# A hybrid state-space and attention kernel: another pacing of the recurrence, and the carry copies on another engine

## The chip, the cores and the metric

The kernel runs on one core of a Trainium2 chip, as one launch. The core has a matrix engine (TensorE, PE in the profile), a vector engine (VectorE, DVE), a scalar engine (ScalarE, ACT), a general one (GpSimd, POOL) and a queue engine (SyncE, SP) that issues most transfers here. [...] The metric is the time of one execution on the device in microseconds (us), as the median over runs. A change of less than 0.5% can't be told from none.

## The reference

The input is eight images of 384 channels and 32 x 32 positions. All arithmetic is in float32. Two layers follow each other.

- Layer 0: an RMS norm over channels, then a selective state-space recurrence over the 1024 positions, once forwards and once backwards, and a 3 x 3 depthwise convolution with a sigmoid gate. The recurrence is `h = dA * h + dBu`, and its output at a position is the sum over 16 states of `h * c`. There are 384 channels x 16 states of it per image and direction.
- Layer 1: a layernorm, causal attention with six heads of 64 over 1024 positions, and, for the first five images only, a second layernorm and a feed-forward part from 384 to 1536 to 384 channels with weights made binary in five groups. Both of its matrix products are scaled by the largest absolute value of the whole image, so the quantised GELU can't begin before the last element of the first product is there.

```
def step(h, inp):
    dA, dBu, c = inp
    h = dA * h + dBu
    return (h, jnp.einsum('bdn,bn->bd', h, c))
```

## The kernel before

**Stages of one image.** `before_scan` (line 308) computes everything that the recurrence reads: norm, input projection (line 342), the short convolution (370 or, on TensorE, 372), the local 3 x 3 convolution with its gates (`local`, 384; `gates`, 445), and `delta` (515), which writes the step sizes and inputs to DRAM. The recurrence follows in slots, and then `attention` (678) and, for five of the images, `feed_forward` (970).

**The recurrence.** It is cut into 768 units, 96 per image: a unit is one group of 128 channels, one half of the positions, one direction and two states. POOL first multiplies the input by the rows of B (`s_first`, line 592). ACT makes the decay factors (line 605), DVE runs two scans of 512 elements (line 610), POOL multiplies the result in place by the rows of C (line 616), and TensorE adds it to a PSUM bank by eight transposing matmuls (line 624). Between the two halves of a direction the last value of each state is carried: the first half copies it into a small tile (line 615), and the second half's scans start from it. So 384 of the 768 units have that copy; before the change POOL makes it, between its two multiplications. POOL's instructions are pinned to program order (`pin`), and a unit's first multiplication is issued two slots ahead of its scans. Six buffers hold `g`.

**The order of the work.** The program is a list of steps, each with a time in us that the author gives it (`Steps`, default 2.5; `@emit.of(...)` sets another). `spread_over` (1084) merges lists in proportion to these times. The tile framework then turns the list into engine queues, with the list's order as priority. The kernel has three parts.

- Part one (0 to 831 us): the input stages of four images and the making of the binary weights, with the first 98 slots spread evenly over them.
- Part two (831 to 4741 us): `rest`, built in lines 1149 to 1158. For each of seven images the attention steps come first. For four of the images a joint list follows: its feed-forward merged with the input stage of a later image, every time multiplied by `JOINT` (0.6). Images 5 and 6 have attention alone. The seventh (image 4) has a feed-forward with no input stage left to merge. Lines 1160 to 1171 then place the slots: each image's 96 slots have to be issued by the end of the stage before its attention, and of the stretches that keep this, the one with the most slots per planned us is taken first, evenly spaced. The planned times therefore decide how many slots fall beside each kind of step; they don't change any step.
- Part three (4741 to 4951 us): the attention of image 7, with no recurrence left.

**The steps that the change touches.** `layernorm` (281) has four steps of 6.0 each. In `attention`, the values (line 745) and the steps of softmax have the default of 2.5: `scores` (773) with the matmuls of line 787, the masking on DVE (801) and the exponential (811), and the steps of `weighted_values` with the transposes (863), their copies (866) and the products with the values (877). There are 36 + 42 = 78 such steps in an image. In `feed_forward`, the two scalings (1011 and 1057) and GELU (1018, 1021) have 3.0 each; TensorE has nothing to do for that image in them.

Of the kernel before, what the change touches and what calls it, by code (L numbers as in the profile page):

```python
# [38 lines left out]
BC0 = 32  # L39
DW = BC0 + 2 * NS  # L40
PARTS = ((0, 0), (0, 1), (1, 1), (1, 0))
JOINT = 0.6
SET = 8
HURRY = 400
AHEAD = 2
# [9 lines left out]
def kernel(  # L55
# [16 lines left out]
    nc = tc.nc  # L72
    pin = tc.keep_in_program_order
# [13 lines left out]
    def btile(name):  # L87
        return big.tile([P, NC, L], F32, name=name, tag="big")
# [16 lines left out]
    def half(h):  # L105
        return slice(h * HB, (h + 1) * HB)
# [153 lines left out]
    def mean_of(c_of, name):  # L260

        m = bank(name)
        for c in range(NC):
            nc.tensor.matmul(out=m, lhsT=onesc, rhs=c_of(c), start=(c == 0), stop=(c == NC - 1))  # L264
        return m
# [6 lines left out]
    def squares(src, h, name):  # L272
        sqs = []
        for c in range(NC):
            if c % 2 == 0:
                sq = mtile(f"sq_{name}_{h}_{c}").rearrange("p (i l) -> p i l", i=2)
            nc.scalar.activation(sq[:, c % 2, :], src[:, c, half(h)], AF.Square)
            sqs.append(sq[:, c % 2, :])
        return sqs

    def layernorm(src, name, emit):

        dst = src
        st = {}
        for h in range(NH):

            @emit.of(6.0)
            def _(h=h):
                mean = mean_of(lambda c: src()[:, c, half(h)], f"mean_{name}_{h}")
                for c in range(NC):  # L290
                    nc.vector.tensor_tensor(
                        dst()[:, c, half(h)], src()[:, c, half(h)], mean, ALU.subtract
                    )
                st[h] = squares(dst(), h, name)

        for h in range(NH):

            @emit.of(6.0)
            def _(h=h):
                var = mean_of(lambda c: st[h][c], f"var_{name}_{h}")  # L300
                rstd_of(var, 1)
                for c in range(NC):
                    nc.vector.tensor_tensor(  # L303
                        dst()[:, c, half(h)], dst()[:, c, half(h)], var, ALU.mult
                    )
# [289 lines left out]
    def s_scan(u):  # L595
        g = sst["g", u.name]
        key = ("carry", u.b, u.c, u.d)
        begins = u.part % 2 == 0
        if begins and u.n == 0:
            sst[key] = sp.tile([P, NS], F32, name=f"carry_{u.name}", tag="carry", bufs=2 * NC)  # L600
        carry = sst[key]
        for i in range(2):
            n = u.n + i
            da = bank(f"da_{u.name}_{i}", "da")
            nc.scalar.activation(  # L605
                da, sst["dl", u.b, u.c, u.part], AF.Exp, scale=amat[:, u.c, n : n + 1]
            )
            first = 0.0 if begins else carry[:, n : n + 1]
            gi, step = g[:, i, :], -1 if u.d else 1
            nc.vector.tensor_tensor_scan(  # L610
                gi[:, ::step], da[:, ::step], gi[:, ::step], first, ALU.mult, ALU.add
            )
        if begins:
            end = 0 if u.d else HB - 1
            pin(nc.gpsimd.tensor_copy(carry[:, u.n : u.n + 2], g[:, :, end]))  # L615
        pin(nc.gpsimd.tensor_tensor(g, g, sst["bc", 1, u.b, u.part, u.n], ALU.mult))  # L616

    def s_sum(u):
# [59 lines left out]
    def attention(b, emit_ffn, emit):  # L678
# [57 lines left out]
                        nc.any.tensor_copy(st["qk"[s]][:, m, half(h)], qp)  # L736
        for j in range(NT):

            @emit
            def _(j=j):  # L740
                if j == 0:
                    st["v"] = btile(f"v_{b}").rearrange("p c l -> p (c l)").rearrange(
                        "p (j e) -> p j e", e=C
                    )
                vp = bank(f"vp_{b}_{j}")
                for c in range(NC):
                    nc.tensor.matmul(  # L747
                        out=vp[:, :C],
                        lhsT=st["xn"][:, c, chunk(j)],
                        rhs=wv[:, c, :],  # L750
                        start=(c == 0),
                        stop=(c == NC - 1),
                    )
                nc.any.tensor_copy(st["v"][:, j, :], vp[:, :C])
# [13 lines left out]
        def probabilities(c, g, steps):  # L768


            nb = g + 1

            def scores(i, qi, n, kb, k0, k1):
                pr = mtile(f"pr_{b}_{c}_{qi}_{kb}").rearrange("p (e l) -> p e l", e=2)
                st["pr", c, g, i, kb] = pr
                if kb == 0 and i == 0:
                    for what in ("nm", "rs"):
                        st[what, c, g] = small.tile(
                            [P, QT, 2, nb], F32, name=f"{what}_{b}_{c}_{g}", tag=f"{what}{nb}"
                        )  # L780
                nm, rs = st["nm", c, g], st["rs", c, g]
                ss = [bank(f"s_{b}_{c}_{qi}_{kb}_{e}", "s") for e in range(2)]

                order = (1, 0)
                for e in order:
                    with at_once(e == order[1]):
                        mm = nc.tensor.matmul(  # L787
                            out=ss[e][:, : k1 - k0],
                            lhsT=st["q"][rows_of(e), c, chunk(qi)],
                            rhs=st["k"][rows_of(e), c, k0:k1],  # L790
                            start=True,
                            stop=True,
                        )
                    if e == order[1]:
                        pin(mm)

                w = k1 - k0
                mask = cmask[:, HB - w :] if k1 == n else cmask[:, :1].to_broadcast([P, w])
                for e in range(2):
                    x, m = pr[:, e, :w], nm[:, i, e, kb : kb + 1]  # L800
                    nc.vector.tensor_tensor_reduce(  # L801
                        out=x,
                        in0=ss[e][:, :w],
                        in1=mask,
                        scale=-1.0,
                        scalar=-MASKED,
                        op0=ALU.add,
                        op1=ALU.min,
                        accum_out=m,
                    )  # L810
                    nc.scalar.activation(  # L811
                        x, x, AF.Exp, bias=m, scale=-1.0, accum_out=rs[:, i, e, kb : kb + 1]
                    )

            for i in range(QT):
                qi = g * QT + i
                n = (qi + 1) * P
                for kb, (k0, k1) in enumerate(blocks_of(n)):
                    steps(lambda i=i, qi=qi, n=n, kb=kb, k0=k0, k1=k1: scores(i, qi, n, kb, k0, k1))

        def weighted_values(c, g, steps):

# [72 lines left out]

            for j in range(last + 1):

                @steps
                def _(j=j):
                    if j == 0:  # L900
                        with tc.high_priority(offset=60):
                            factors()
                    if j % QT == QT - 1:
                        spread(j // QT)
                    turned(j)
                    if j > 0:
                        weigh(j - 1)

            @steps
            def _():  # L910
                weigh(last)

# [57 lines left out]
    def feed_forward(b, t, emit):  # L970
# [35 lines left out]
                            st["mxh"][:, m : m + 1], hm, AX.X, ALU.max, apply_absolute_value=True  # L1006
                        )

        @emit.of(3.0)
        def _():  # L1010
            st["s1"] = quant_scale(st["mxh"], f"h_{b}")


        @emit.of(3.0)
        def _():
            with tc.high_priority(offset=60):
                for q in range(NF // NC):
                    pin(nc.scalar.activation(st["h", q], st["h", q], AF.Gelu, scale=st["s1"]))
                pin(nc.scalar.preload_act_table_set(LOG_EXP))
                for q in range(NF // NC):  # L1020
                    nc.vector.tensor_scalar(st["h", q], st["h", q], QCLIP, None, ALU.min)  # L1021
# [30 lines left out]
                            st["mxy"][:, m : m + 1], ym, AX.X, ALU.max, apply_absolute_value=True  # L1052
                        )

        @emit.of(3.0)
        def _():
            st["s2"] = quant_scale(st["mxy"], f"y_{b}")

# [16 lines left out]
    class Steps(list):  # L1075
# [4 lines left out]

        def of(self, us):
            return lambda f: self(f, us)

    def spread_over(*lists):

# [64 lines left out]
    for i, b in enumerate(ORDER):  # L1150
        if i > 0:
            due.append((sum(us for _, us in rest), i * per))
        fed = Steps()
        rest += steps_of(attention, b, fed) if i < B - 1 else []
        if fed and later:
            fed = spread_over(fed, steps_of(before_scan, later.pop(0), ("pt", "pt", "av")))
            fed = [(f, JOINT * us) for f, us in fed]
        rest += fed

    timed, here = [], 0  # L1160
# [63 lines left out]
```

## Time and profile before

| | |
|---|---|
| Median of 3 runs | 4947.5 us (4943.6 to 4969.1) |
| Profiled execution: time, span | 4952.4 us, 4950.6 us |
| Granted TensorE clock, mean | 0.885 |
| Busy: PE, DVE, ACT, POOL | 81%, 74%, 54%, 75% |
| A joint stage, mean of four | 324.5 us |
| An attention stage with the recurrence beside it | 329 to 357 us |
| The last attention, without it | 210 us |
| The last feed-forward (image 4) | 212 us |

The profile is of one execution. A row of it names the line, the engine, the operation, what it writes and reads and how often it ran; then come the busy time in us and the mean of one in ns; then how long the engine was idle just before, and who ended that idle time. An answer by windows gives, for each stretch of time, its length and the busy us of each engine in it with the number of instructions. Busy time of PE is of pipelined matmuls whose ends are modelled.

### The profile page before, as it was taken

The numbers are of one execution on the slowest core, as the hardware profiler recorded it, in microseconds if no ns is written. First come the engines' busy times: TensorE is split into PE (matmuls) and PEld (weight loads), VectorE is DVE, ScalarE is ACT, GpSimd is POOL, SyncE is SP. The second block draws the span as 40 slices with busy tenths as digits, with TensorE's granted clock in tenths as the row PEclk, the third lists the DMA queues.
The fourth block names the chain that finished last, engine by engine and source line by source line (L and its number), as shares of the span: only waits on it lengthen the run. The fifth ranks groups of instructions, "written<-read, shape, count | busy, mean of one in ns | idle before, by whom it ended". The sixth has DMA issues, their size and how long they took to land. (4 is left out here: it accounts for less than half of the span.)

```text
span 4950.6 us, 50616 instructions
## 1 busy us (share of the span) xinstructions
PE 4007.3 (81%) x16362; PEld 2168.0 (44%) x16362; DVE 3659.0 (74%) x4818; ACT 2669.5 (54%) x4855; POOL 3696.7 (75%) x1944
## 2 busy tenths in 40 slices
PE   4677786988788788688887888887887988988889
PEld 1243343544444444344443444443454444444444
DVE  6887878677887778786778967687867677676623
ACT  4565655564654655545655446565456365464425
POOL 0487787996878986768876699867799888888800
PEclk7787796999989899888898998898899989989999
DMA  6554546333454334363343634334643334334210
GB/s 228 204 177 165 196 157 238 107 102 124 150 198 137 115 124 165 126 207 114 108 135 128 220 121 135 111 128 153 203 128 119 114 112 140 117 103 139 92 61 26
DMA packets 365009, 696.35 MB, mean 141 GB/s; under 512 B 30104, under 2 KB 88904, under 8 KB 364744
## 3 DMA queue, kind: packets, MB, share of 16 engines
q1 hardware_dynamic: 355232, 676.97, 41.4%
q10 hardware_dynamic: 9512, 16.15, 0.9%
q8 instruction: 129, 2.11, 0.2%
q14 instruction: 136, 1.11, 0.1%
HBM read 527.33 MB, written 165.68 MB: 140 GB/s over the span
## 5 line engine op out<-in xcount | busy, mean ns | idle before, releaser
L592 POOL TENSOR_TENSOR g<-ud,bc 128x1024 f32<-128x1024 f32 x768 | 1843.2, 2400 | 518.7 <-PE y L624 391.9
L616 POOL TENSOR_TENSOR g<-g,bc 128x1024 f32<-128x1024 f32 x768 | 1821.0, 2371 | 271.1 <-DVE g L610 196.1
L605 ACT ACTIVATE da<-dl,amat 128x512 f32<-128x512 f32 x1536 | 1056.9, 691 | 1457.7 <-DVE g L610 1436.7
L610 DVE TENSOR_TENSOR_SCAN g<-da,g 128x512 f32<-128x512 f32 x768 | 907.5, 1211 | 423.5 <-POOL g L592 411.8
L610 DVE TENSOR_TENSOR_SCAN g<-da,carry,g 128x512 f32<-128x512 f32 x768 | 953.7, 1272 | 348.4 <-POOL g L592 322.9
L624 PE MATMUL y<-ident,g 128*128 128x128 f32 x6144 | 938.7, 301 | 249.2 <-POOL g L616 122.2
L624 PEld LDWEIGHTS y<-ident,g 128*128 128x128 f32 x6144 | 782.0, 155 | 696.7 <-issue 379.8
L787 PE MATMUL s<-k,q 64*128 64x512 f32 (+3 forms) x1152 | 388.4, 600 | 121.6 <-DVE nm L801 103.5
L801 DVE CUSTOM_DVE_ANT_0 pr<-s,cmask 128x512 f32<-128x512 f32 (+3 forms) x576 | 300.3, 546 | 168.4 <-PE s L787 167.1
L811 ACT ACTIVATE pr<-pr,nm 128x512 f32<-128x512 f32 (+3 forms) x576 | 349.9, 609 | 123.6 <-DVE nm L801 121.9
L863 PE MATMUL pt<-ident,pr 128*128 128x128 f32 x1728 | 301.9, 307 | 98.1 <-ACT ptn L866 78.5
L995 PE MATMUL hp<-t,w 128*128 128x512 f32 x720 | 335.7, 611 | 38.7 <-DMA w<-w1s 30.8
L1039 PE MATMUL yp<-h,w 128*128 128x512 f32 x720 | 331.7, 619 | 19.2 <-DMA w<-w2s 15.1
L863 PEld LDWEIGHTS pt<-ident,pr 128*128 128x128 f32 x1728 | 216.2, 154 | 240.2 <-ACT ptn L866 134.5
L877 PE MATMUL av<-ptn,v 128*64 128x512 f32 (+3 forms) x1152 | 270.8, 551 | 49.7 <-ACT ptn L866 35.8
L342 PE MATMUL in<-xn,win 128*128 128x512 f32 x576 | 282.7, 637 | 26.8 <-DVE xc L464 8.2
L866 ACT COPY ptn<-pt 128x512 f32<-128x512 f32 (+3 forms) x576 | 255.6, 474 | 62.0 <-PE pt L863 60.0
L401 DVE SCALAR_TENSOR_TENSOR loc<-xn,vec,loc 128x496 f32<-128x496 f32 (+3 forms) x384 | 259.6, 722 | 20.1 <-ACT loc L390 18.8
L729 PE MATMUL qp<-t,wqk 128*128 128x512 f32 x576 | 263.3, 607 | 10.3 <-DVE t L303 6.5
L615 POOL COPY carry<-g 128x2 f32<-128x2 f32 x384 | 85.7, 223 | 214.8 <-DVE g L610 214.6
L787 PEld LDWEIGHTS s<-k,q 64*128 64x128 f32 x1152 | 132.2, 207 | 257.9 <-DVE nm L801 174.9
L1039 PEld LDWEIGHTS yp<-h,w 128*128 128x128 f32 x720 | 141.8, 201 | 194.0 <-issue 169.8
(151 smaller groups left out, 4714.2 us busy)
## 6 DMA issues: line engine op xcount, KB each, us to landing
bc<-rows SPq DMA_DIRECT2D x512, 512.0 KB, 4.2
dl<-sdl SPq DMA_DIRECT2D x160, 256.0 KB, 3.0
ud<-sud SPq DMA_DIRECT2D x160, 256.0 KB, 2.8
t<-st SPq DMA_DIRECT2D x63, 512.0 KB, 5.0
su<-u SPq DMA_DIRECT2D x48, 512.0 KB, 4.0
du<-su SPq DMA_DIRECT2D x96, 256.0 KB, 3.9
sdl<-du SPq DMA_DIRECT2D x96, 256.0 KB, 2.6
sud<-du SPq DMA_DIRECT2D x96, 256.0 KB, 2.2
```

The lines of the kernel that those rows point to most:

```text
L342: nc.tensor.matmul(out=mp, lhsT=st["win", c][:, k, i, :], rhs=st["xn"][:, k, half(h)], start=(k == 0), stop=(k == NC - 1),)
L592: pin(nc.gpsimd.tensor_tensor(g, ud, sst["bc", 0, u.b, u.part, u.n], ALU.mult))
L605: nc.scalar.activation(da, sst["dl", u.b, u.c, u.part], AF.Exp, scale=amat[:, u.c, n : n + 1])
L610: nc.vector.tensor_tensor_scan(gi[:, ::step], da[:, ::step], gi[:, ::step], first, ALU.mult, ALU.add)
L616: pin(nc.gpsimd.tensor_tensor(g, g, sst["bc", 1, u.b, u.part, u.n], ALU.mult))
L624: nc.tensor.matmul(out=y[:, j, :], lhsT=g[:, i, chunk(j)], rhs=ident, is_transpose=True, start=(u.opens and i == 0 and j == 0), stop=(u.cl ...
L787: mm = nc.tensor.matmul(out=ss[e][:, : k1 - k0], lhsT=st["q"][rows_of(e), c, chunk(qi)], rhs=st["k"][rows_of(e), c, k0:k1], start=True, st ...
L801: nc.vector.tensor_tensor_reduce(out=x, in0=ss[e][:, :w], in1=mask, scale=-1.0, scalar=-MASKED, op0=ALU.add, op1=ALU.min, accum_out=m,)
L811: nc.scalar.activation(x, x, AF.Exp, bias=m, scale=-1.0, accum_out=rs[:, i, e, kb : kb + 1])
L863: nc.tensor.transpose(pt[:, chunk(i)], pr[:, e, chunk(j % QT)], ident)
L995: nc.tensor.matmul(out=hp, lhsT=st["w1"][:, c, chunk(m % 2)], rhs=st["xn"][:, c, half(h)], start=(c == 0), stop=(c == NC - 1),)
L1039: nc.tensor.matmul(out=yp, lhsT=st["w2", k // 6][:, k % 6, :], rhs=st["h", k // NC][:, k % NC, half(h)], start=(k == 0), stop=(k == NF - 1),)
```

## The change

The planned times are set anew, and one copy moves.

- `JOINT` is 1.0 instead of 0.6, so a joint list counts with its full planned time.
- The steps of softmax are planned at 1.6 instead of 2.5, the values at 2.0 instead of 2.5, the layernorm steps at 3.0 instead of 6.0.
- The two scalings and GELU are of a new type `Gap`, with 9, 16 and 9 instead of 3 each. In a joint list these times are used when the feed-forward and the input stage are merged; after that each counts as `SHORT`, 3.0, in the placing of slots. In the last feed-forward they count in full.
- The copy of the carried values is issued to VectorE instead of GpSimd, and isn't pinned to program order there.

```diff
-JOINT = 0.6
+JOINT = 1.0
+SHORT = 3.0
...
-            @emit.of(6.0)
+            @emit.of(3.0)
             def _(h=h):
                 mean = mean_of(lambda c: src()[:, c, half(h)], f"mean_{name}_{h}")
...
-            @emit.of(6.0)
+            @emit.of(3.0)
             def _(h=h):
                 var = mean_of(lambda c: st[h][c], f"var_{name}_{h}")
...
             end = 0 if u.d else HB - 1
-            pin(nc.gpsimd.tensor_copy(carry[:, u.n : u.n + 2], g[:, :, end]))
+            nc.vector.tensor_copy(carry[:, u.n : u.n + 2], g[:, :, end])
         pin(nc.gpsimd.tensor_tensor(g, g, sst["bc", 1, u.b, u.part, u.n], ALU.mult))
...
-            @emit
+            @emit.of(2.0)
             def _(j=j):
                 if j == 0:
                     st["v"] = btile(f"v_{b}").rearrange("p c l -> p (c l)").rearrange(
...
-                    steps(lambda i=i, qi=qi, n=n, kb=kb, k0=k0, k1=k1: scores(i, qi, n, kb, k0, k1))
+                    steps(lambda i=i, qi=qi, n=n, kb=kb, k0=k0, k1=k1: scores(i, qi, n, kb, k0, k1), 1.6)
...
-                @steps
+                @steps.of(1.6)
                 def _(j=j):
...
-            @steps
+            @steps.of(1.6)
             def _():
                 weigh(last)
...
-        @emit.of(3.0)
+        @emit.of(Gap(9.0))
         def _():
             st["s1"] = quant_scale(st["mxh"], f"h_{b}")
...
-        @emit.of(3.0)
+        @emit.of(Gap(16.0))
         def _():
             with tc.high_priority(offset=60):
                 for q in range(NF // NC):
...
-        @emit.of(3.0)
+        @emit.of(Gap(9.0))
         def _():
             st["s2"] = quant_scale(st["mxy"], f"y_{b}")
...
+    class Gap(float):
+        pass
+
...
-            fed = [(f, JOINT * us) for f, us in fed]
+            fed = [(f, JOINT * (SHORT if isinstance(us, Gap) else us)) for f, us in fed]
         rest += fed
```

## The prediction

> **What bounds the kernel now.** I read the page's first two parts, then busy time by stage, then the softmax stretches, then single rows. The page says that no engine is full over the span:
>
> ```profile
> PE 4007.3 (81%) x16362; PEld 2168.0 (44%) x16362; DVE 3659.0 (74%) x4818; ACT 2669.5 (54%) x4855; POOL 3696.7 (75%) x1944
> ```
>
> So the stages differ. With the stages cut at the first and last out-projection matmuls of each image (lines 699, 937), three windows show the two kinds and the attention that runs with no recurrence beside it (columns: PE, PEld, DVE, ACT, POOL busy us, then granted clock, DMA share, GB/s):
>
> ```profile
> 1486.00:1830.00 344.00, 285.92 (x1376) 162.18 (x1376) 252.18 (x365) 186.63 (x396) 303.21 (x156) 0.91 0.39 128
> 1830.00:2159.00 329.00, 258.17 (x873) 134.88 (x872) 265.28 (x291) 183.61 (x266) 226.74 (x118) 0.88 0.47 153
> 4741.00:4951.00 210.00, 199.70 (x864) 95.41 (x864) 66.12 (x201) 98.06 (x258) 0.00 (x0) 0.98 0.09 35
> ```
>
> Attention (first line) has POOL at 0.88 and DVE at 0.73; the joint stage (second) has DVE at 0.81, PE 0.78, POOL only 0.69. The softmax part shows the first more sharply, with and without the recurrence:
>
> ```profile
> 1590.00:1810.00 220.00, 175.55 (x1004) 103.99 (x1004) 163.76 (x270) 139.36 (x320) 199.00 (x109) 0.88 0.35 114
> 4815.00:4933.00 118.00, 112.54 (x652) 55.31 (x652) 48.19 (x175) 81.30 (x228) 0.00 (x0) 0.99 0.04 14
> ```
>
> POOL is at 0.90 there and PE at 0.80: softmax is paced by POOL's two multiplications per unit. The four joint stages together, and the rows of a unit:
>
> ```profile
> sum 1298.00, PE 1042.46 PEld 544.05 DVE 1063.82 ACT 726.89 POOL 916.58; mean PE 260.61 PEld 136.01 DVE 265.95 ACT 181.72 POOL 229.15
> ```
>
> ```profile
> L592 POOL TENSOR_TENSOR g<-ud,bc 128x1024 f32<-128x1024 f32 x768 | 1843.2, 2400 | 518.7 <-PE y L624 391.9
> L616 POOL TENSOR_TENSOR g<-g,bc 128x1024 f32<-128x1024 f32 x768 | 1821.0, 2371 | 271.1 <-DVE g L610 196.1
> L610 DVE TENSOR_TENSOR_SCAN g<-da,g 128x512 f32<-128x512 f32 x768 | 907.5, 1211 | 423.5 <-POOL g L592 411.8
> L610 DVE TENSOR_TENSOR_SCAN g<-da,carry,g 128x512 f32<-128x512 f32 x768 | 953.7, 1272 | 348.4 <-POOL g L592 322.9
> L615 POOL COPY carry<-g 128x2 f32<-128x2 f32 x384 | 85.7, 223 | 214.8 <-DVE g L610 214.6
> L1021 DVE TENSOR_SCALAR h<-h 128x3072 f32<-128x3072 f32 x20 | 64.2, 3253 | 4.3 <-ACT h L1018 4.3
> ```
>
> A unit costs POOL 2.400 + 2.371 = 4.77 us, DVE 1.211 + 1.272 = 2.48 plus 0.14 (rows of lines 645, 671, 672: 105.8 us over 768), 2.62 in all, and PE about 1.2 (joint windows of line 624: 240 us for 200 units).
>
> [...] line 837, with 16 elements and two SBUF inputs, runs 174 ns at least and 2001 at the median:
>
> ```profile
> L837 DVE TENSOR_TENSOR rs<-rs,nm x24: 174/2001/2215, 980.9 to 4918.2; 128x16 f32<-128x16 f32 x24
> ```
>
> and line 1021 (one source, SBUF to SBUF) is 1735 ns at its shortest against a mean of 3253. No run here shows a two-element DVE copy.
>
> **The change part by part.** *The plan.* A slot of the recurrence is set per so much planned step time. Before, attention sums to 306.5, a joint list to 0.6 x (181.6 + 180.2) = 217.1, the last feed-forward to 181.6. The steepest stretch is 576 slots over 2707.3: 4.70 a slot, 65 units in attention and 46 in a joint stage; the windows of line 592 count 64 to 66 and 46 to 48, so the plan is what runs. After, softmax is 78 x 1.6 = 124.8 instead of 195, values 16 instead of 20, layernorm 12 instead of 24: attention 220.3; a joint list is 169.6 + 180.2 = 349.8; the last feed-forward 194.6. Now one stretch covers all, 672 slots over 3135.9, 4.667 a slot: **47 units in attention, 75 in a joint stage**, 26.7 instead of 41.5 in softmax.
>
> *Softmax.* PE's own 112.54 at clock 0.99 is 126.6 at 0.88; 26.7 units x 1.29 (windows of line 624 in the seven stretches: 370.1 us for 288 units) add 34.4: 161. POOL needs 26.7 x 4.77 = 127, so PE paces. PE reached 0.95 alone; I take 0.90 because DVE still interrupts: 179. The seven stretches average 216.7, so 7 x 38 = **-266** (0.95 gives -330, 0.85 gives -191). Outside softmax 3.2 fewer units x 1.3 x 7 = **-28**, PE being the bound there already.
>
> *Joint stages.* 28.5 units more. DVE: 266 + 28.5 x 2.62 = 341. POOL: 75 x 4.77 = 358. PE: 261 + 34 = 295. Two engines are now near full where none was.
>
> *The copies.* POOL loses 384 x 0.223 = 86 us, already in the 4.77. DVE gains 384 copies. Unblocked I take 0.15, near line 837's 0.174. Blocked, it waits for the POOL multiplication that is running, on average half of 2.36, so 0.15 + 0.85 x 1.18 = 1.15 with POOL at 0.85. The ends are 0.15 and 2.5; none of it can be a gain on DVE. Per joint stage, 37.5 x 1.15 = 43: DVE 384. Behind the copy on DVE stand the next scans, the local convolution's taps and the score masks, and PE waits for those masks. POOL's second multiplication now waits for the copy as it did for its own; 0.15 against 0.223, no gain counted. Where DVE would have waited for line 592 anyway, the block is hidden; where DVE has other work queued, it isn't.
>
> *The sum for a joint stage.* Best shares seen: POOL 0.93 in one softmax stretch, DVE 0.94 in one 100 us window. 384 / 0.92 = 417 against 324.5: 4 x 93 = **+371**. The ends: POOL alone at 0.93 and cheap copies, 385, +242; DVE at 0.85, 452, +510.
>
> *Gap filling.* In joint lists the gaps of 9, 16 and 9 only shift the input stage's steps towards GELU and count 3 in pacing. In the last feed-forward, 6 more units x 1.2 / 0.84 = +9, less PE idle between lines 995 (ends 4634) and 1039 (from 4653): **+5** (-5 to +15). *First 831 us*: 48 copies x 1.15 = 55 on a DVE at 0.82, a quarter of it felt: **+14** (0 to 40). *Transfers.* 28.5 units carry 19 loads of bc and 12 of dl and ud, about 13 MB; 51 MB in 325 us become 64 in 417, the same rate, so nothing. Weight loads queue behind them on SP; lines 995 and 1039 waited 46 us for weights in all, and that may grow.
>
> Sum: -266 - 28 + 371 + 5 + 14 = +96. The profiled execution took 4952.4 (span 4950.6 and 1.8 around it), 4.9 above the median of 4947.5: 5048 on its scale, **5040** on the median's, rounded.
>
> **Rivals.** (1) *Joint stages stay POOL-paced, faster.* Copies fall into DVE's existing waits for line 592 (735 us in all) and POOL holds 0.93: 385 each. -294 + 242 + 5 + 0 = -47: 4900. It decides below 324.5 + (294 - 19) / 4 = 393 per joint stage. For it: DVE does wait for POOL today. Against: POOL is at 0.70 there because DVE bursts hold the scans; from 2085 to 2159 DVE is busy 69.8 of 74 us and POOL 47.0. (2) *A wash*: joint stages near 393: 4947. (3) *DVE saturates*: 452 each, softmax gains only 191: +510 - 219 + 15 + 40 = +346: 5290. For it: the burst just named; against: half of the units have no copy. (4) *The pacing isn't followed*: unlikely, since counts match the plan.
>
> **How the numbers follow.** Mine 0.55 (own range 4985 to 5190), rival 1 0.22, rival 2 0.10, rival 3 0.13. Slower 0.68, same 0.10, faster 0.22, with 0.5% as what a measurement can tell. The range 4885 to 5200 reaches into rival 1 and leaves about 0.1 on each side.
>
> **What would show it.** Line 592 counts 47 and 75 by stage; softmax stretches near 179 with PE at 0.90 and POOL near 0.71; joint stages near 417 with DVE and POOL both over 0.85; a DVE copy row of 384 with a mean near 1.15 us and a minimum near 0.15. Copies at 0.15 throughout, or joint stages under 393, make me wrong; so does a softmax stretch that stays above 200.

## The result and the profile after

The changed kernel takes 5071.8 us at the median of four runs (5066.6 to 5075.3), the kernel before 4945.6 (4933.9 to 4969.1). The ratio is 1.0251, with a 95% interval from 1.0221 to 1.0281: slower by 2.5%, where 1.9% was forecast. The profiled execution took 5068.9 us, with a span of 5067.1.

The page of the kernel after begins with the busy time of the engines:

```profile
PE 4057.6 (80%) x16362; PEld 2173.5 (43%) x16362; DVE 3954.5 (78%) x5194; ACT 2700.3 (53%) x4880; POOL 3624.6 (72%) x1560
```

DVE is busy 295 us longer than before, POOL 72 us less (its copies took 86). The groups of the recurrence (one constant was added at the top, so line 592 of before is 593 here, 616 is 617, and so on):

```profile
L593 POOL TENSOR_TENSOR g<-ud,bc 128x1024 f32<-128x1024 f32 x768 | 1849.8, 2409 | 756.7 <-PE y L625 558.9
L617 POOL TENSOR_TENSOR g<-g,bc 128x1024 f32<-128x1024 f32 x768 | 1823.7, 2375 | 449.6 <-DVE carry L616 192.3
...
L611 DVE TENSOR_TENSOR_SCAN g<-da,g 128x512 f32<-128x512 f32 x768 | 909.0, 1208 | 190.5 <-POOL g L593 183.8
...
L616 DVE COPY carry<-g 128x2 f32<-128x2 f32 x384 | 385.1, 1003 | 6.1
```

The 384 copies of two elements take 385 us, 1.003 us each, more than the whole rise, since some other rows of DVE are shorter than before. POOL's second multiplication waits 192 us for them, but this is mostly not their length: POOL's own copy had waited 214.6 us for the scans before it. The scans without a carry waited 411.8 us for POOL before and wait 183.8 now: DVE comes to them later.

The second image's attention stage and joint stage, as in the prediction (columns again PE, PEld, DVE, ACT and POOL busy, the granted clock, DMA share, GB/s):

```profile
1530.00:1852.00 322.00, 271.40 (x1272) 148.03 (x1272) 235.19 (x369) 169.62 (x369) 240.80 (x103) 0.91 0.35 115
1852.00:2256.00 404.00, 306.32 (x1072) 164.79 (x1071) 358.65 (x373) 219.78 (x319) 336.70 (x143) 0.84 0.48 158
```

Attention gained 22 us and has no engine over 0.85; the joint stage lost 75, with DVE at 0.89 and POOL at 0.83. One softmax stretch, and the four joint stages in sum:

```profile
1649.00:1831.00 182.00, 151.07 (x867) 84.64 (x867) 132.67 (x258) 116.06 (x283) 123.28 (x54) 0.91 0.29 93
```

```profile
sum 1623.00, PE 1234.02 PEld 672.33 DVE 1458.68 ACT 882.96 POOL 1353.96; mean PE 308.50 PEld 168.08 DVE 364.67 ACT 220.74 POOL 338.49
```

Softmax fell to 182 us, PE at 0.83 of it and POOL at 0.68. Line 593 runs 46 to 51 times in an attention stage and 71 to 73 times in a joint stage.

All stage lengths below are cut at the same out-projection matmuls, from the traces (us). Attention is the seven stages beside the recurrence, softmax the part of them from the first score to the last transpose; ratios are to the kernel before, with 95% intervals. The last attention, 204 to 206 us in each of these traces, is left out. Stage lengths are of one execution of each kernel, which can lie some way from the median that the ratio rests on (before_reduce: 4940 us profiled, 4962 at the median), so differences of a few us between rows say nothing. The rows below the second are the experiments'.

| kernel | part one | attention | of it softmax | four joint | last feed-forward | ratio |
|---|---|---|---|---|---|---|
| before | 831 | 2404 | 1513 | 1295 | 211 | 1 |
| after | 842 | 2173 | 1268 | 1623 | 220 | 1.0251 (1.0221 to 1.0281) |
| copy_dve_only | 839 | 2447 | 1538 | 1292 | 215 | 1.0126 (1.0098 to 1.0154) |
| pacing_only | 827 | 2120 | 1237 | 1598 | 216 | 1.0040 (1.0026 to 1.0055) |
| after_reduce | 836 | 2123 | 1234 | 1596 | 214 | 1.0049 (1.0033 to 1.0065) |
| before_reduce | 831 | 2403 | 1516 | 1284 | 211 | 1.0017 (1.0002 to 1.0033) |
| lock_attention | 834 | 2169 | 1264 | 1595 | 214 | 1.0162 (1.0145 to 1.0179) |
| lock_joint | 831 | 2125 | 1233 | 1622 | 214 | 1.0111 (1.0085 to 1.0137) |
| gap3_reduce | 833 | 2131 | 1248 | 1605 | 215 | 1.0098 (1.0066 to 1.0130) |
| joint06 | 840 | 2311 | 1381 | 1380 | 236 | 1.0060 (1.0037 to 1.0083) |
| joint06_reduce | 837 | 2252 | 1334 | 1367 | 229 | 0.9858 (0.9824 to 0.9891) |
| best | 832 | 2287 | 1416 | 1319 | 215 | 0.9841 (0.9824 to 0.9859) |

### The profile page after: what moved, and what is told of

The parts are those of the page before. It is cut to its first block, busy times and chain, and to the rows that moved or that the text cites. A ratio compares the mean times of both kernels' runs of the same rounds, so it can differ in the third digit from the quotient of the medians.

```text
span 5067.1 us, 50844 instructions
## 1 busy us (share of the span) xinstructions
PE 4057.6 (80%) x16362; PEld 2173.5 (43%) x16362; DVE 3954.5 (78%) x5194; ACT 2700.3 (53%) x4880; POOL 3624.6 (72%) x1560
## 3 DMA queue, kind: packets, MB, share of 16 engines
q14 instruction: 138, 1.13, 0.1%
## 5 line engine op out<-in xcount | busy, mean ns | idle before, releaser
L611 DVE TENSOR_TENSOR_SCAN g<-da,g 128x512 f32<-128x512 f32 x768 | 909.0, 1208 | 190.5 <-POOL g L593 183.8
L788 PE MATMUL s<-k,q 64*128 64x512 f32 (+3 forms) x1152 | 373.8, 580 | 94.6 <-DVE nm L802 86.7
L812 ACT ACTIVATE pr<-pr,nm 128x512 f32<-128x512 f32 (+3 forms) x576 | 350.9, 610 | 129.2 <-DVE nm L802 127.0
L996 PE MATMUL hp<-t,w 128*128 128x512 f32 x720 | 358.8, 639 | 44.2 <-DMA w<-w1s 21.8
L616 DVE COPY carry<-g 128x2 f32<-128x2 f32 x384 | 385.1, 1003 | 6.1
L1040 PE MATMUL yp<-h,w 128*128 128x512 f32 x720 | 345.2, 636 | 10.1 <-DMA w<-w2s 10.1
L788 PEld LDWEIGHTS s<-k,q 64*128 64x128 f32 x1152 | 131.5, 198 | 231.7 <-DVE nm L802 167.3
```

The lines of the kernel that those rows point to most:

```text
L611: nc.vector.tensor_tensor_scan(gi[:, ::step], da[:, ::step], gi[:, ::step], first, ALU.mult, ALU.add)
L616: nc.vector.tensor_copy(carry[:, u.n : u.n + 2], g[:, :, end])
L788: mm = nc.tensor.matmul(out=ss[e][:, : k1 - k0], lhsT=st["q"][rows_of(e), c, chunk(qi)], rhs=st["k"][rows_of(e), c, k0:k1], start=True, st ...
L812: nc.scalar.activation(x, x, AF.Exp, bias=m, scale=-1.0, accum_out=rs[:, i, e, kb : kb + 1])
L996: nc.tensor.matmul(out=hp, lhsT=st["w1"][:, c, chunk(m % 2)], rhs=st["xn"][:, c, half(h)], start=(c == 0), stop=(c == NC - 1),)
L1040: nc.tensor.matmul(out=yp, lhsT=st["w2", k // 6][:, k % 6, :], rhs=st["h", k // NC][:, k % NC, half(h)], start=(k == 0), stop=(k == NF - 1),)
```

## The experiments

The theory to be tested is that of the prediction: the new pacing moves units from attention into the joint stages until these lose more than softmax gains, and the copies add to it there. The rivals are that the loss is the pacing alone, or the copies alone.

**The copies alone, and the pacing alone.** The first is the kernel before with the copy on DVE:

```diff
-            pin(nc.gpsimd.tensor_copy(carry[:, u.n : u.n + 2], g[:, :, end]))
+            nc.vector.tensor_copy(carry[:, u.n : u.n + 2], g[:, :, end])
```

> The kernel before with the carry copies on VectorE and nothing else. Theory (the pacing makes most of the loss, the copies the rest): 1.003 to 1.012 of before; a copy row of 384 with a mean near 1.0 us, DVE busy up by about 385 us, POOL busy down by about 86 us; units by stage stay near 65 and 47. Rival 1 [...]: 1.02 or more. Rival 2 (the copies hide, the relief of POOL shows): 0.993 to 1.002, with softmax stretches shorter by 5 us or more, since POOL paces them.

The second is the kernel after with the copy put back on POOL:

```diff
-            nc.vector.tensor_copy(carry[:, u.n : u.n + 2], g[:, :, end])
+            pin(nc.gpsimd.tensor_copy(carry[:, u.n : u.n + 2], g[:, :, end]))
```

> The changed kernel with the carry copies back on POOL, in program order. Theory: 1.012 to 1.022 of before; joint stages near 390 to 400 with 71 to 75 units, softmax stretches near 175 to 180. Rival 1 (copies make the loss): 0.985 to 0.998, joint stages under 385. Rival 2 (copies cost nothing): 1.025 or above, joint stages 405 or more, since POOL then carries 0.22 us more for every second unit.

Measured: 1.0126 and 1.0040. The copies cost 1.3% with the old pacing, just above what the theory said, and the pacing 0.4%, far less than the 1.2 to 2.2% that I expected of it, and less than the 0.5% that can be told from none. The stages of pacing_only did come out as expected (joint stages of 399 us at the mean, softmax stretches of 177); the total that I had set beside them was wrong. The copy's group in copy_dve_only:

```profile
L615 DVE COPY carry<-g 128x2 f32<-128x2 f32 x384 | 399.4, 1040 | 6.1
```

The table puts its loss into attention (+43 us, more than half of it in softmax), and none into the joint stages (-3). The two losses sum to 1.7%, the whole change costs 2.5%: the copies cost more with the new pacing. So the copy is the larger part, and the pacing without it is near a wash.

**Is it the lock, or the place of the copy?** "The lock" is my name for a wait that the traces show: a DVE instruction begins while a POOL instruction runs and lasts until that one ends. The trace of before has it in line 837: 21 of its 24 instructions began while a POOL instruction ran and took 1.11 to 2.22 us, and all 21 ended within 0.06 us of the end of that instruction; the other three took 0.174 to 0.176 us. Not every DVE operation does so: of the 48 small reductions of lines 834 and 838, 37 began while a POOL instruction ran, and none took over 171 ns. The same value can be moved by a reduction over one element, an operation that writes the same bits into the same tile at the same place of DVE's queue. That it wouldn't wait was an estimate, which those 37 support; why one operation waits and another doesn't, no run shows. The reduction was run with the new pacing and with the old (the same edit of the kernel before, in place of POOL's copy):

```diff
-            nc.vector.tensor_copy(carry[:, u.n : u.n + 2], g[:, :, end])
+            nc.vector.tensor_reduce(
+                carry[:, u.n : u.n + 2], g[:, :, end : end + 1], AX.X, ALU.max
+            )
```

> The changed kernel with each carry copy written as a max-reduction over one element per state, still on VectorE: the same two values[...]. If the wait of a copy is the lock against a running POOL multiplication, its mean falls from 1.00 to 0.13 to 0.20 us with a maximum under 0.5, and DVE busy falls by about 310 us; if the wait is something else (the scan's result, a full queue), the mean stays near 1.0. On the time: theory 1.013 to 1.021 of before (the pacing's part stays); rival 1 (copies make the loss) under 1.0; rival 2 (copies cost nothing) 1.025.

> The kernel before with each carry copy written as a max-reduction over one element on VectorE, nothing else. It differs from copy_dve_only by the lock alone and from the kernel before by the relief of POOL. Theory now (the lock is what a copy on VectorE costs; it hurts where score masks stand behind it): 0.995 to 1.002 of before, a copy row near 0.15 us, attention stages back at or under those of before (mean 342 us), and POOL busy down by 86 us. Rival (the place in DVE's queue costs, not the lock): 1.008 or more, near copy_dve_only's 1.0126.

The instructions of that line in after (first) and in after_reduce (second), with the shortest, median and longest duration in ns:

```profile
L616 DVE COPY carry<-g x384: 134/685/6880, 140.8 to 4703.3; 128x2 f32<-128x2 f32 x192
```

```profile
L616 DVE TENSOR_REDUCE carry<-g x384: 124/154/169, 138.7 to 4615.0; 128x2 f32<-128x2 f32 x192
```

No reduction took over 169 ns beside a POOL that is 73% busy. Of the copies in after, 137 began while POOL was idle, and none of these took over 171 ns. The other 247 began while a POOL instruction ran; 239 of them took over 200 ns, and 235 of these ended within 0.06 us of the end of that instruction.

The time goes from 5071.8 to 4977.4 us (1.0251 to 1.0049), 94 us, which is outside what I expected of after_reduce (1.013 to 1.021). With the old pacing the reduction gives 1.0017, against 1.0126 for the copy. So the lock costs 2.0 points with the new pacing and 1.1 with the old. The place in DVE's queue and the 86 us that POOL no longer spends on copies come together to nothing that can be told (1.0017 against before; 1.0049 against the 1.0040 of pacing_only). No run separates the two, so a small cost of the one could hide a small gain of the other.

One block can be watched in the timeline of after, in softmax (start, duration in us, engine, instruction; in brackets the idle time before it and who ended it). DVE first, then POOL and PE:

```profile
1735.74 0.66 DVE L802 CUSTOM_DVE_ANT_0 pr<-s,cmask 128x512 f32<-128x512 f32 x1
...
1736.33 2.19 DVE L616 COPY carry<-g 128x2 f32<-128x2 f32 x1
1738.43 0.68 DVE L802 CUSTOM_DVE_ANT_0 pr<-s,cmask 128x512 f32<-128x512 f32 x1
```

```profile
1736.14 2.35 POOL L617 TENSOR_TENSOR g<-g,bc 128x1024 f32<-128x1024 f32 x1
```

```profile
1739.17 1.64 PE L788 MATMUL s<-k,q 64*128 64x384 f32 x2 [1.58 <-DVE nm L802]
```

POOL's multiplication starts at 1736.14 and ends at 1738.49; the copy comes 0.19 us after that start and ends at 1738.52. The score mask behind it starts about 2.0 us later than behind a reduction of 0.15 us, and the next scores on PE have waited 1.58 us for it. The rows of the scores in after and in after_reduce:

```profile
L788 PE MATMUL s<-k,q 64*128 64x512 f32 (+3 forms) x1152 | 373.8, 580 | 94.6 <-DVE nm L802 86.7 <-ACT v L755 4.5 <-DVE v L755 1.1
L788 PEld LDWEIGHTS s<-k,q 64*128 64x128 f32 x1152 | 131.5, 198 | 231.7 <-DVE nm L802 167.3 <-issue 41.6 <-DVE g L611 8.0
```

```profile
L790 PE MATMUL s<-k,q 64*128 64x512 f32 (+3 forms) x1152 | 367.4, 571 | 82.7 <-DVE nm L804 73.5 <-ACT v L757 4.5 <-DVE carry L616 2.1
L790 PEld LDWEIGHTS s<-k,q 64*128 64x128 f32 x1152 | 130.4, 196 | 217.6 <-DVE nm L804 153.1 <-issue 37.9 <-DVE g L611 8.5
```

PE's scores and their weight loads wait 254.0 us for the masks in after (86.7 + 167.3) and 226.6 in after_reduce (73.5 + 153.1), where the attention stages differ by 50 us; the exponentials on ACT wait 127.0 and 99.8. Waits of PE and of its weight loads can overlap, so the sums show the direction, not the whole of the loss.

**Where the lock costs.** The copy on DVE in the attention stages only, or in the joint stages only, and the reduction elsewhere (the mark is set by the first step of `attention` and of `feed_forward`; lock_joint asks for "joint"):

```diff
+            if where[0] == "attention":
+                nc.vector.tensor_copy(carry[:, u.n : u.n + 2], g[:, :, end])
+            else:
+                nc.vector.tensor_reduce(
```

> [...] The changed kernel has 148 us of copies in those stages and 178 in the joint ones, but its stages are longer than after_reduce's by about 50 us in attention and 27 in the joint stages. Theory (a blocked copy costs where score masks stand behind it and TensorE waits for them): 1.013 to 1.017 of before, attention stages longer than after_reduce's by 40 to 60 us in sum, joint stages within 10. Rival (a blocked copy costs in proportion to the time it is blocked): 1.010 to 1.013.

> [...] Theory: 1.008 to 1.012 of before, joint stages longer by 20 to 35 us in sum. Rival (in proportion to blocked time): 1.013 to 1.016, joint stages longer by 45 us or more; what the prediction charged to the joint stages was 113.

The groups of the copy in lock_attention (first) and lock_joint:

```profile
L618 DVE COPY carry<-g 128x2 f32<-128x2 f32 x164 | 146.7, 895 | 2.9
```

```profile
L618 DVE COPY carry<-g 128x2 f32<-128x2 f32 x155 | 179.4, 1157 | 2.0
```

The ratios rise over that of after_reduce by 1.13 points for attention and by 0.62 for the joint stages, both as the theory said and not in proportion to the blocked time. In the traces only the stage with the copy grows: attention by 46 us, the joint stages by 26. The scores and their weight loads wait 249.7 us for the masks in lock_attention and 225.2 in lock_joint, against 226.6 in after_reduce. Set against the blocked time (the row less 0.15 us a copy), 122 us in attention and 156 in the joint stages, attention feels 38% of it and a joint stage 17%. The blocks are longer in a joint stage, and cost less.

**How many units the joint stages should get.** JOINT back to 0.6, with the copy and with the reduction:

```diff
-JOINT = 1.0
+JOINT = 0.6
```

> The changed kernel with JOINT at 0.6 instead of 1.0. Planned: attention 220.3, joint 209.9, last feed-forward 194.6, 3.83 a slot; 57 or 58 units in attention (33 in softmax), 55 in a joint stage, 51 in the last feed-forward. Theory (the loss comes from units beyond what a joint stage can carry): 0.975 to 0.995 of before, joint stages 340 to 360, softmax stretches 185 to 200. Rival 1 (the copies' lock makes the loss): 1.015 or more. Rival 3 (softmax units cost the same wherever they are put, so only their number counts): 1.00 to 1.01.

> joint06 with the copies as reductions: both causes eased at once. Planned 58 to 59 units in attention (33 in softmax) and 56 in a joint stage. Theory (the loss is the lock plus too many units in joint stages): 0.982 to 0.992 of before, softmax stretches 185 to 195, joint stages 335 to 345. Rival (moving units between stages gains nothing wherever they go): 0.998 to 1.005.

Measured: 1.0060 and 0.9858. The second is what I expected. The first missed its 0.975 to 0.995. Its joint stages came out in the expected band and its softmax stretches just above it (188 to 203 us against 185 to 200), but the copies, at 1128 ns each, took the gain: the reduction alone makes 2.0 points. The last feed-forward rose to 236 us with 38 units beside it (29 before); the expectation had counted 51 there, because it left out that the slots of the last images are placed at another rate than the first. The new planned times of softmax are thus worth keeping when the joint stages count as before: 55 units in a joint stage instead of 72 give 342 us (joint06_reduce) instead of 399 (after_reduce).

**The gap filling.** The three `Gap` steps back to 3.0, on after_reduce:

```diff
-        @emit.of(Gap(9.0))
+        @emit.of(3.0)
...
-        @emit.of(Gap(16.0))
+        @emit.of(3.0)
...
-        @emit.of(Gap(9.0))
+        @emit.of(3.0)
```

> after_reduce with the two scalings and GELU planned at 3.0 each as before, so that the feed-forward's gap is not filled. The prediction put the gap filling at -10 to +10 us in the whole. Theory: within 15 us of after_reduce's 4977 (1.002 to 1.008 of before); the joint stages change by under 4 us each. Rival (the filled gap shortens each joint stage by the idle of TensorE around GELU): 1.012 or more.

Measured 1.0098, 4998 us against after_reduce's 4977: 21 us, a little over the 15 of the expectation. The planned times of the gaps are worth about half a per cent, at the limit of what can be told. The two traces are 15 us apart, with 8 us in attention and 9 in the joint stages, 2 each. The edit also moves units, because the gaps count in full in the last feed-forward: it has 30 units beside it instead of 35 and is no shorter (215 against 214 us), while the joint stages have three more and attention two. Units that cost nothing there are then as good a reason as a filled gap; no run separates the two.

**What paces a joint stage without the lock?** A kernel that leaves out five of the eight off-centre taps of the local 3 x 3 convolution, and so a part of what layer 0 computes, on after_reduce. It was to spare DVE 21.7 us in each joint stage:

```diff
-                if k == 4:
+                if k in (0, 2, 4, 5, 6, 8):
```

> after_reduce with five of the eight off-centre taps of the local convolution left out (so part of layer 0's local branch is missing): VectorE has 30 fewer of its 0.72 us taps in a joint stage, 21.7 us, with 75 units planned as before. It tells what holds a joint stage at POOL 0.85 and DVE 0.84. Theory (VectorE's bursts hold the scans, so both engines bound it by turns): joint stages shorter by 10 to 22 us from a mean of 399, POOL at 0.88 or more. Rival (POOL paces the joint stage once it has 71 units): shorter by under 6 us. The first 831 us shorten too and are not part of the reading.

It was run once: 4910.8 us. The joint stages go from 1596 to 1577, 4.7 us each. The sums of the joint stages in after_reduce and in taps3:

```profile
sum 1595.00, PE 1223.17 PEld 668.77 DVE 1334.58 ACT 880.85 POOL 1352.04; mean PE 305.79 PEld 167.19 DVE 333.64 ACT 220.21 POOL 338.01
```

```profile
sum 1579.00, PE 1223.83 PEld 679.00 DVE 1289.26 ACT 872.58 POOL 1360.38; mean PE 305.96 PEld 169.75 DVE 322.32 ACT 218.15 POOL 340.10
```

The relief of DVE was smaller than meant: its busy time falls by 11.3 us a stage, not by 21.7. The taps take 20.3 us less, but the additions of line 440 take 14.4 us a stage instead of 9.2; the longest took 9.0 us, the shortest 1.2. (In the trace of after, the five of these 24 additions beside which POOL was idle took 1.23 us at most, and the 17 that began while a POOL instruction ran 1.46 to 5.41 us.) So a joint stage gave back less than half of what DVE was spared. DVE alone doesn't pace it, but DVE isn't without effect either.

POOL is the fullest, at 0.85 and 0.86 of the stage. In the second joint stage of after_reduce it is idle for 56 us, and the largest single part of that is 16 us of waiting for scans. That POOL paces the stage is the better reading, but what keeps it at 0.85 instead of the 0.90 it had in softmax before stays open. More buffers for `g` would test one answer; that wasn't tried. Part one shortened by 39 us (836 to 797) for 120 taps fewer.

**Between the two pacings.** On joint06_reduce, softmax steps at 2.0:

```diff
-                    steps(lambda i=i, qi=qi, n=n, kb=kb, k0=k0, k1=k1: scores(i, qi, n, kb, k0, k1), 1.6)
+                    steps(lambda i=i, qi=qi, n=n, kb=kb, k0=k0, k1=k1: scores(i, qi, n, kb, k0, k1), 2.0)
...
-                @steps.of(1.6)
+                @steps.of(2.0)
...
-            @steps.of(1.6)
+            @steps.of(2.0)
```

> joint06_reduce with the softmax steps planned at 2.0 instead of 1.6: 62 units in attention (38 in softmax), 51 to 52 in a joint stage. By the prediction's prices POOL and TensorE are even in softmax at about 36 units, so the best lies near here: theory 0.980 to 0.992 of before, within 0.4% of joint06_reduce. Rival (TensorE still paces softmax at 33 units, so fewer is better): slower than joint06_reduce by 0.5% or more.

> joint06_soft2_reduce again, for a profile and a tighter interval: 0.981 to 0.987 of before. By the plan 62 units in attention and 51 to 52 in a joint stage; softmax stretches 195 to 205 with POOL and TensorE both between 0.82 and 0.88; joint stages 325 to 340.

The same kernel, measured twice: 0.9833 (0.9798 to 0.9868, three runs) and 0.9841 (four runs), 4873 us. It beats both kernels; from joint06_reduce it can't be told apart. Its softmax stretches took 188 to 208 us, with PE at 0.81 and POOL at 0.87, a little off the expected bands. The page of best, and its joint stages:

```profile
PE 3974.7 (82%) x16362; PEld 2141.7 (44%) x16362; DVE 3699.4 (76%) x5205; ACT 2688.3 (55%) x4868; POOL 3614.3 (74%) x1560
```

```profile
sum 1320.00, PE 1077.20 PEld 560.70 DVE 1115.79 ACT 765.70 POOL 966.32; mean PE 269.30 PEld 140.17 DVE 278.95 ACT 191.43 POOL 241.58
```

It has 50 to 52 units in a joint stage (DVE at 0.85, POOL 0.73) and 37.7 at the mean in a softmax stretch. Before it was 41.0: the first 3.3 units taken out shorten the stretch by 13.9 us, 4.2 us each, near the price of a unit on POOL (4.77). From there to the 26.7 of after_reduce it shortens by 26 us more, only 2.4 a unit, and PE is the fullest engine at the end (0.84, POOL 0.71); the joint stages pay 3.3 us for each unit that they get beyond 51 (69 us for 21 units).

## Why the prediction was right and where it wasn't

The direction and the place were right: softmax shortens, the joint stages pay more than that, and the copy of two elements costs about a microsecond. The terms below are between the profiled executions, 5067 and 4951 us long. Term by term, in us:

| term | predicted | after | after_reduce (no lock) |
|---|---|---|---|
| softmax, seven stretches | -266 | -245 | -279 |
| attention outside softmax | -28 | +14 | -2 |
| joint stages | +371 | +328 | +301 |
| gap filling (last feed-forward) | +5 | +9 | +3 |
| part one | +14 | +11 | +5 |
| sum | +96 | +117 | +27 |

**Pacing and units.** Followed: 47 and 75 units were predicted, 46 to 51 and 71 to 73 counted. By these counts about three units that the plan puts into a joint stage run in the attention after it.

**Softmax.** 179 us predicted, 181 measured. PE reached 0.83 instead of the 0.90 I took, with less PE work than I had counted (150.6 instead of 161 us a stretch); the two errors cancel, which is luck. The clock may be part of the second, which no run tests: I had scaled PE's work to the 0.88 granted before, by estimate, and these stretches were granted 0.92 at the mean.

**Outside softmax.** This step failed: -28 became +14. The plan takes 3.2 units out of each stage here, 22 in all, but 153 ran there after the change and 156 before: units spilled from the joint stages fall here. So nothing was gained even without the lock (-2), and the lock costs another 16.

**The copies.** The price was near, 1.15 predicted and 1.003 measured, with the shortest at 134 ns and the longest, 6.88 us, beyond the 2.5 that I gave as the end. That a copy of two elements would wait for POOL at all was an estimate: no run had such a copy on DVE, and the trace of before had the wait in line 837. Its placing was wrong. I charged 113 us to the joint stages (417 with the copies against 389 without, four times), 14 to part one and nothing to attention, 127 in all. The lock cost 94 at the medians and 90 between the traces: 50 in attention, 27 in the joint stages, 6 each in part one and the last feed-forward. The prediction had named the masks behind the copy and PE behind the masks, and then put no term for attention into the sum. In the joint stages it added the whole copy to DVE's work as if DVE paced them; lock_joint shows 17% of the block felt, and in taps3 4.7 us are felt of the 11.3 that DVE was spared.

**The pace of a joint stage.** Without the copies, the prediction's own arithmetic makes POOL the fuller engine, and 358 / 0.92 = 389. Measured 399, with 338 us of POOL work in it: a share of 0.85. The 0.92 was near the best shares seen in shorter windows; a whole stage with POOL at 0.85 and DVE at 0.84 didn't hold it. The stage also had three units fewer than planned, 338 us of POOL work instead of 358, which hides part of this error. What is left is 43 us in four stages (+258 against +301). The granted clock fell too, from 0.88 to 0.84 in the joint stage shown; no run separates what that costs.

So the sum of 96 against 117 is better than its parts, by luck. Without the lock my terms give -266 - 28 + 258 + 5 = -31, and +27 was measured: the pacing alone was priced 58 us too well, the lock 33 us too dear. By these terms the copies made the whole loss and the pacing a gain; when I expected most of the loss of the pacing in the experiments, I overlooked that. Two of the products are a microsecond or two off (7 x 37.7 is 264, 3.2 x 1.3 x 7 is 29), which changes nothing. Rival 1, joint stages paced by POOL and faster, had the right engine, but not the 385 us: 399 even without the lock is beyond the 393 from which it was to decide. That the rate of the transfers stays was right: DMA moved 158 GB/s in the joint stage shown, 153 before, and the waits for weights in the feed-forward (lines 996 and 1040) fell from 46 to 32 us.

## What to carry to other kernels

A small DVE copy from SBUF to SBUF was priced here by what GpSimd was running, not by its size: 171 ns at most for the 137 that began while GpSimd was idle, 1513 ns on average for the 239 that took over 200. Where GpSimd is busy, try another operation that moves the same value, here a reduction over one element at 150 ns instead of 1003. Price the wait by who stands behind it in each stage, since the same block cost twice as much of its length in attention as in the joint stages. And when work is moved between stages, price it per unit and stop where the stage that gives no longer gains the full price of its bound engine.

## What the runs showed of the hardware that was not expected

- Of the 384 copies in after, 145 took under 200 ns and 239 were longer, 1513 ns on average. Four took over 2400 ns, longer than the POOL multiplication that ran when they began. In the longest, 6.88 us, the copy starts at 3634.07 and ends at 3640.95, and POOL runs three multiplications back to back over it (timeline of after, DVE and then POOL):

```profile
3634.07 6.88 DVE L616 COPY carry<-g 128x2 f32<-128x2 f32 x1
```

```profile
3633.94 2.36 POOL L593 TENSOR_TENSOR g<-ud,bc 128x1024 f32<-128x1024 f32 x1
3636.26 2.34 POOL L617 TENSOR_TENSOR g<-g,bc 128x1024 f32<-128x1024 f32 x1
3638.56 2.36 POOL L593 TENSOR_TENSOR g<-ud,bc 128x1024 f32<-128x1024 f32 x1
3641.08 2.35 POOL L617 TENSOR_TENSOR g<-g,bc 128x1024 f32<-128x1024 f32 x1 [0.16 <-POOL g L593]
```

  It gets through at the first gap of POOL, 0.16 us. So the end of one multiplication need not let the copy in, though it did for 235 of the 239: my upper bound of 2.5 us, the rest of one instruction, was not a bound. The 6.40 us copy at 1938.24 shows the same, with three multiplications without a gap and the same 0.16 us after them.
- With 86 us less work on POOL, the engine at 0.90 in softmax before, and 57 us of reductions on DVE in its place, nothing was gained (before_reduce: softmax 1516 against 1513). A likely reason is that the copy had stood on POOL where POOL would mostly have waited for the scans anyway: the row of line 615 before has 214.6 us of waiting for them. No run tested it.
- POOL's own copy of two elements, in the kernel before, took 186 ns at the median and 1711 at its longest. 25 of the 384 took over 400 ns, and each of these ended within 0.06 us of the end of a DVE instruction (lines 530, 532 and 1021) that was running when it began.
